# One Trainium2 core, sparse attention by its leading entries: row factors by root and reciprocal, a column number that carries its own skip, whole-block searches, a wider table, wider late segments

## The chip, the cores and the metric

The kernel runs on one core of a Trainium2 chip. The metric is the time of one execution on the device in microseconds (us). Before the change the median of three executions is 234.67 us (234.59 to 234.72).

## What is computed

The reference adds a four-head graph attention to `x` and normalises each row:

```python
ht = (h @ W).reshape(N, 4, 512).transpose(1, 0, 2)
e = jax.nn.leaky_relu(src[:, :, None] + dst[:, None, :], 0.01) + adj_mat[None]
att = jax.nn.softmax(e, axis=-1)
return jnp.einsum('hij,hjd->hid', att, ht).mean(axis=0)
...
x = _layernorm(x + _L0_gnn_ref(x, adj, W, a), axis=-1)
```

Here `x` is 4096 x 512, `adj` is 4096 x 4096 with entries up to 1e9, and `W` is 512 x 2048, all in 32-bit floats. The entries of `adj` are so large that the softmax of a row has all its weight on the column of the row's largest entry. So the attention of row i is row j of `x` times the mean of the four heads of `W`, where j is that column; the kernel computes just that, tests at the end whether the gaps to the second largest entries are wide enough for it, and would run a general version (`general`) if one were not.

## The kernel before the change

The 4096 rows are worked on in 32 blocks of 128, numbered 0 to 31. In the loop over `t` (lines 523 to 584) each turn issues work for several blocks in different stages, all engines have their program written out by hand in this order, and each engine works through its own list in that order.

- SyncE's DMA queue loads `adj` block by block (2 MB each, line 127), five blocks ahead, into six buffers, with the loads of `x` (line 134) between them; a buffer is free when VectorE has searched it. The stores of the result follow at the end (line 430).
- VectorE, for block t: `segment_maxima` (line 203) takes the maximum of each segment of 16, 32 or 64 columns, as two reductions of 2048 columns each; `find_segment` (lines 210 and 212) finds the row's largest segment and its number `at`. GpSimd adds the row's offset (`row`, line 219), fetches that one segment of `adj` again (`lead`, line 223, an indirect DMA) and multiplies the number by the segment's width (`start`, line 230).
- VectorE, for block t - 2: `find_column` (lines 257 and 263) looks for the maximum within the fetched segment. GpSimd forms the column number (`col`, line 265) and gathers the 128 rows of `x` that it names (`y`, lines 239 and 248, an indirect DMA). In the turns of the tuple `END` (1, 2 and 5 to 19) `find_column` stands behind `find_segment`, in the others between the two halves of the segment search.
- Blocks 1 to 17 are `TABLED`: rows of `x` below 128 are not gathered. Their products lie in a table that was computed once, and a one-hot matrix `pick` (`spread`, lines 324 to 328) selects them on TensorE. For such a block GpSimd adds 8192 to column numbers below 128 (`away`, `there`, lines 245 and 247), which puts them outside the bounds of the gather, so that they are skipped, and ScalarE has cleared the block beforehand.
- TensorE, for block t - 3: the gathered rows are transposed (`tp`, line 277), ScalarE copies them (`yt`, line 279), and TensorE adds the residual (line 289), the table's part (line 336) and the product with the mean of the heads (line 296).
- ScalarE, for block t - 4: the square sum of a row of `x` (`row_norm`, line 340) and the sums for mean and variance (`parked_stats`, lines 361 and 363).
- Every fourth turn from t = 8 on, `rstd` makes the factors of four blocks, t - 8 to t - 5, on GpSimd: a multiply and add, the power -0.5 (line 367), and two more products. ScalarE's `finish` (line 375) applies them a turn or more later.

So at turn t the factors need the sums of block t - 5, which ScalarE forms in its turn t - 1, behind the copy of the transposed rows of block t - 4. Those rows were gathered in turn t - 2.

From block 24 (`BEHIND`) on the results are put by, and finished after the loop (lines 586 to 652); the last blocks are normalised on VectorE with batch statistics (`moments`, `factor`, `normalise`). `head_norms` (lines 453 to 473), in turns 24, 26 and 28, computes norms for the final test, with a PSUM tile `px` that has one buffer and that `spread` uses as well.

## Time and profile before

| what | before |
|---|---|
| median of three runs | 234.67 us |
| the profiled execution: its time | 234.5 us |
| its span in the trace | 233.0 us |
| VectorE busy | 191.1 us (82%) |
| TensorE busy | 194.3 us (83%) |
| ScalarE busy | 139.8 us (60%) |
| GpSimd busy | 112.9 us (48%) |
| moved by DMA | 96.45 MB, mean 414 GB/s |

The trace gives each instruction a start and a duration, counted from the start of the span. Behind an instruction that found its engine idle stand, in square brackets, the length of that idle time and what ended it. Some 1.5 us of the execution lie outside the span. PE is TensorE, PEld its weight loads, DVE is VectorE, ACT is ScalarE, POOL is GpSimd, SP is SyncE.

### The profile page before, as it was taken

Reading aid. Unit: us, or ns where it says so; the run is one execution under the profiler, and the core shown is the slowest. Engines: PE = TensorE matmul, PEld = TensorE weight load, DVE = VectorE, ACT = ScalarE, POOL = GpSimd, SP = SyncE. Lnnn points to the kernel's source line nnn. Section 1 sums busy time; section 2 is a strip of 40 time slices with the busy share of each in tenths; the row PEclk is TensorE's granted clock in tenths of the full one; section 3 lists DMA queues with packets and bytes.
Section 4 is the critical chain, followed back from the end, with each engine's and each line's share of the span. In section 5 each row is a group of like instructions: output and inputs, shape, how many; then the busy total and the mean of one; then the engine's idle time right before and its main releaser. Section 6 shows DMA issues by size and latency. Waiting matters only on the chain.

```text
span 233.0 us, 2399 instructions
## 1 busy us (share of the span) xinstructions
PE 194.3 (83%) x570; PEld 92.6 (40%) x576; DVE 191.1 (82%) x301; ACT 139.8 (60%) x340; POOL 112.9 (48%) x260
## 2 busy tenths in 40 slices
PE   0069988789099996999899999999999977899990
PEld 0024443334044443445344444544443433345460
DVE  0448299899969997999799958977999999988782
ACT  3002213588077775699798767767756763289761
POOL 4020415615554875467657755653465447557210
PEclk9999999999769998899999999999999999999998
DMA  6999999999999999999999999999999999999985
GB/s 229 433 422 437 420 437 421 438 427 414 436 431 420 422 433 434 427 421 434 423 426 424 432 429 427 420 430 430 429 432 413 427 422 425 410 425 418 424 357 203
DMA packets 12834, 96.45 MB, mean 414 GB/s; under 512 B 2087, under 2 KB 2535, under 8 KB 7056
## 3 DMA queue, kind: packets, MB, share of 16 engines
q1 hardware_dynamic: 9216, 88.08, 89.5%
q0 software_dynamic: 3584, 8.16, 8.9%
q8 instruction: 5, 0.08, 0.1%
q14 instruction: 13, 0.11, 0.1%
q10 hardware_dynamic: 16, 0.02, 0.0%
HBM read 88.54 MB, written 8.39 MB: 416 GB/s over the span
## 4 chain that ended last, share of the span: by engine, by line
DMA 64%; DVE 19%; PE 6%; ACT 4%; issue 3%; POOL 1%; SPq 0%; DVEq 0%; POOLq 0%
DMA adj_t<-in_adj_dram 56%; DVE seg L203 16%; DMA hold<-in_L_gnn_W_dram 5%; PE o L296 4%; DMA y<-in_x_dram,col 3%; ACT sq L340 2%; PE o L384 2%; DVE at L212 1%; ACT hold L375 1%; DVE top L210 1%; PE tp L277 1%; DVE within L263 1%; POOL sd L367 0%; POOL lead L223 0%; ACT yt L279 0%
## 5 line engine op out<-in xcount | busy, mean ns | idle before, releaser
L203 DVE TENSOR_REDUCE seg<-adj_t 128x128 f32<-128x2048 f32 (+3 forms) x66 | 144.1, 2210 | 29.8 <-DMA adj_t<-in_adj_dram 29.7
L296 PE MATMUL o<-w_sum,yt 128*128 128x512 f32 x248 | 114.4, 602 | 2.0 <-ACT yt L279 1.8
L296 PEld LDWEIGHTS o<-w_sum,yt 128*128 128x128 f32 x248 | 46.3, 193 | 54.9 <-issue 42.6
L279 ACT COPY yt<-tp 128x512 f32<-128x512 f32 x33 | 19.1, 579 | 34.3 <-PE tp L277 34.3
L223 POOL DMA_INDIRECT lead<-in_adj_dram,row x32 | 32.6, 1020 | 13.1 <-POOL row L219 13.1
L277 PE MATMUL tp<-ident,y 128*128 128x128 f32 x128 | 22.5, 300 | 15.9 <-DMA y<-in_x_dram,there 12.0
L219 POOL TENSOR_TENSOR row<-at,first 128x1 uint32<-128x1 uint32 x32 | 6.1, 191 | 54.0 <-DVE at L212 45.4
L277 PEld LDWEIGHTS tp<-ident,y 128*128 128x128 f32 x128 | 18.7, 208 | 30.5 <-issue 27.0
L435 PE MATMUL o<-hold,ident 128*128 128x512 f32 x32 | 17.0, 699 | 13.7 <-DMA hold<-in_L_gnn_W_dram 13.7
L289 PE MATMUL o<-hold,ident 128*128 128x512 f32 x52 | 27.5, 614 | 0.0
L248 POOL DMA_INDIRECT y<-in_x_dram,there x17 | 18.9, 1111 | 10.9 <-POOL there L247 5.6
L340 ACT ACTIVATE sq<-hold 128x512 f32<-128x512 f32 x32 | 19.9, 624 | 0.0
L375 ACT ACTIVATE hold<-hold,nm,sd 128x512 f32<-128x512 f32 x24 | 19.1, 802 | 0.0
L239 POOL DMA_INDIRECT y<-in_x_dram,col x15 | 14.9, 995 | 7.6 <-POOL col L265 7.0
L363 ACT ACTIVATE sq<-hold,nm 128x512 f32<-128x512 f32 x24 | 17.4, 724 | 0.8
L435 PEld LDWEIGHTS o<-hold,ident 128*128 128x128 f32 x32 | 7.1, 226 | 22.8 <-issue 22.3
L436 ACT ACTIVATE w_sum<-o 128x512 f32<-128x512 f32 x4 | 2.4, 597 | 22.9 <-PE o L435 22.9
L326 ACT ACTIVATE off<-px,minus 128x128 f32<-128x128 f32 x17 | 6.3, 368 | 15.3 <-PE px L324 15.3
L361 ACT ACTIVATE hold<-o 128x512 f32<-128x512 f32 x24 | 14.3, 597 | 0.8
L336 PE MATMUL o<-z,pick 128*128 128x512 bf16 x46 | 13.9, 407 | 0.2
L210 DVE MAX8 top<-seg 128x8 f32<-128x256 f32 (+2 forms) x32 | 11.6, 361 | 1.1
L212 DVE FIND_INDEX8 at<-top,seg 128x8 uint32<-128x256 f32 (+2 forms) x32 | 11.3, 352 | 0.0
(113 smaller groups left out, 178.7 us busy)
## 6 DMA issues: line engine op xcount, KB each, us to landing
adj_t<-in_adj_dram SPq DMA_DIRECT2D x28, 2048.0 KB, 33.0
hold<-in_x_dram SPq DMA_DIRECT2D x6, 1024.0 KB, 32.4
adj_t<-in_adj_dram SPq DMA_DIRECT2D x6, 1024.0 KB, 28.1
hold<-in_L_gnn_W_dram SPq DMA_DIRECT2D x2, 2048.0 KB, 16.6
out_dram<-hold SPq DMA_DIRECT2D x7, 512.0 KB, 5.4
out_dram<-hold SPq DMA_DIRECT2D x3, 1024.0 KB, 15.1
adj_t<-in_adj_dram SPq DMA_DIRECT2D x4, 512.0 KB, 19.8
hold<-in_x_dram SPq DMA_DIRECT2D x2, 512.0 KB, 14.4
```

What stands on the lines that cost most here:

```text
L203: nc.vector.tensor_reduce(seg_of[ib][:, ts(k, N // e // n)], adj_t[ib][:, ts(k, N // n)].rearrange("p (s e) -> p s e", e=e), axis=AX.X, op ...
L223: nc.gpsimd.indirect_dma_start(out=lead, out_offset=None, in_=adj_segs[e], in_offset=bass.IndirectOffsetOnAxis(ap=row[:, :1], axis=0),)
L239: nc.gpsimd.indirect_dma_start(out=y, out_offset=None, in_=x, in_offset=bass.IndirectOffsetOnAxis(ap=col[:, :1], axis=0),)
L248: nc.gpsimd.indirect_dma_start(out=y_t[ib], out_offset=None, in_=x, in_offset=bass.IndirectOffsetOnAxis(ap=there[:, :1], axis=0), bounds_c ...
L277: nc.tensor.transpose(tp[:, kb, :], y[:, ds(kb, P, KB)], ident)
L279: nc.scalar.copy(yt, tp)
L289: nc.tensor.matmul(o_ps[ib], ident, hold[:, ib, :], start=start, stop=False)
L296: nc.tensor.matmul(o_ps[ib], yt_of[ib][:, kb, :], w_sum[:, kb, :], start=(start and kb == 0), stop=(kb == KB - 1),)
L340: nc.scalar.activation(sq, hold[:, ib, :], AF.Square, accum_out=xx[:, ib : ib + 1])
L363: nc.scalar.activation(sq, hold[:, ib, :], AF.Square, bias=nm[:, i], scale=-float(D), accum_out=sd[:, i])
L375: nc.scalar.activation(hold[:, ib, :], o, AF.Identity, bias=nm[:, i], scale=sd[:, i])
L435: nc.tensor.matmul(o, ident, hold[:, w_at + kb * H + h, :], start=(h == 0), stop=(h == H - 1))
```

## The change

It has six parts.

1. The factors (`rstd`): ScalarE takes the root (`root`, a new function, issued at the end of turn t - 1 for the factors of turn t), VectorE the reciprocal (in place of GpSimd's power, at the place where `rstd` stood), and GpSimd keeps the two products. The same holds for the last call of `rstd`, after the loop.
2. The skip of tabled blocks is added to the segment's start (in `fetch_segment`), so that `col` is the gather's index as it stands.
3. `END` reaches to turn 27, and in its turns the segment search is one reduction of all 4096 columns.
4. The table serves blocks 1 to 20.
5. Segments are 64 columns wide from block 24 (before: from block 28).
6. `head_norms` is called in turns 21, 22 and 23.

```diff
-LAST = 4
+LAST = 8
-TABLED = range(1, 18)
+TABLED = range(1, 21)
...
-    LEADS = (8, 8, LAST)
+    LEADS = (8, 4, LAST)
...
-    nc.gpsimd.iota(nth, pattern=[[0, 1]], base=0, channel_multiplier=-1)
+    nc.gpsimd.iota(nth, pattern=[[0, 1]], base=-1, channel_multiplier=-1)
...
-        n = max(pieces(ib), 2)
+        n = max(pieces(ib), 1 if ib in END else 2)
...
-            nc.gpsimd.tensor_tensor(start, at[:, 0:1], width[:, k : k + 1], op=OP.mult)
+            if ib in TABLED:
+                away = small.tile([P, 1], F32, name="away")
+                nc.gpsimd.tensor_scalar(away, at[:, 0:1], float(P // e), float(SKIP), op0=OP.is_lt, op1=OP.mult)
+                nc.gpsimd.tensor_scalar(start, at[:, 0:1], float(e), away, op0=OP.mult, op1=OP.add)
+            else:
+                nc.gpsimd.tensor_tensor(start, at[:, 0:1], width[:, k : k + 1], op=OP.mult)
...
-        away = small.tile([P, 1], U32, name="away")
-        nc.gpsimd.tensor_scalar(away, col, float(P), float(SKIP), op0=OP.is_lt, op1=OP.mult)
-        there = small.tile([P, 1], U32, name="there")
-        nc.gpsimd.tensor_tensor(there, col, away, op=OP.add)
...
+    def root(i):
+        nc.scalar.activation(sd[:, i], sd[:, i], AF.Sqrt, bias=eps, scale=1.0 / D)
+
     def rstd(i):
-        nc.gpsimd.tensor_scalar(sd[:, i], sd[:, i], 1.0 / D, EPS, op0=OP.mult, op1=OP.add)
-        nc.gpsimd.tensor_tensor(sd[:, i], sd[:, i], power[:, : i.stop - i.start], op=OP.pow)
+        nc.vector.reciprocal(sd[:, i], sd[:, i])
         nc.gpsimd.tensor_mul(nm[:, i], nm[:, i], sd[:, i])
...
-    END = (*range(1, 3), *range(5, 20))
+    END = (*range(1, 3), *range(5, 28))
...
-        middle = 1 if t == NB - 1 else 2
+        middle = PIECES if t in END else 1 if t == NB - 1 else 2
...
-        segment_maxima(t, middle, PIECES)
+        if t not in END:
+            segment_maxima(t, middle, PIECES)
...
-        if t in (24, 26, 28):
-            head_norms((t - 24) // 2)
+        if 21 <= t < 24:
+            head_norms(t - 21)
...
+        if FINISH <= t + 1 < NB and (t + 1) % Q == 0:
+            root(slice(t + 1 - FINISH, t + 1 - FINISH + Q))
...
     stats(BEHIND + 2)
+    root(slice(BEHIND, BEHIND + 3))
     rstd(slice(BEHIND, BEHIND + 3))
```

What the change does to the engines' lists is seen best at three places. The first is VectorE's list around turn 12: `seg` are the segment maxima of a block, `lead` the fetched segment of the block two before. Before the change it reads:

```order
L203 TENSOR_REDUCE seg_796<-adj_t 128x128 x2
L210 MAX top<-seg_796 128x8
L212 MAX_INDEX at<-top,seg_796 128x8
L257 MAX inner<-lead_683 128x8
L263 MAX_INDEX within<-top,lead_683 128x8
L203 TENSOR_REDUCE seg_860<-adj_t 128x128 x2
```

After the change, at the same place:

```order
L201 TENSOR_REDUCE seg_772<-adj_t 128x256
L208 MAX top<-seg_772 128x8
L210 MAX_INDEX at<-top,seg_772 128x8
L256 MAX inner<-lead_663 128x8
L262 MAX_INDEX within<-top,lead_663 128x8
L368 RECIPROCAL sd<-sd 128x4
L201 TENSOR_REDUCE seg_832<-adj_t 128x256
```

The two reductions of a block have become one, and the reciprocal of four blocks' roots stands ahead of the next block's reduction.

The second place is ScalarE's list, where the root of those factors is made; `sq,sd` are the square sums of block 7. Before the change:

```order
L279 COPY yt<-tp 128x512
L444 ACTIVATE sq,ww<-hold 128x512
L340 ACTIVATE sq,xx<-hold 128x512
L361 ACTIVATE hold,nm<-o 128x512
L363 ACTIVATE sq,sd<-hold,nm 128x512
L375 ACTIVATE hold<-hold,nm,sd 128x512
```

After the change:

```order
L278 COPY yt<-tp 128x512
L445 ACTIVATE sq,ww<-hold 128x512
L339 ACTIVATE sq,xx<-hold 128x512
L360 ACTIVATE hold,nm<-o 128x512
L362 ACTIVATE sq,sd<-hold,nm 128x512
L365 ACTIVATE sd<-sd,eps 128x4
L376 ACTIVATE hold<-hold,nm,sd 128x512
```

The root stands behind the square sums of block 7 and so behind the copy of the transposed rows of block 8, in ScalarE's turn 11.

The third place is TensorE's list in turn 21, after the change, with the semaphores that its rows wait for: the two products of `head_norms` and, behind them, block 18's `spread`.

```order
L295 MATMUL o<-w_sum,yt 128x512 x3
L460 MATMUL px<-ww,ones 128x16
L461 MATMUL px<-each,ones 128x8 [waits DVE_49]
L323 LDWEIGHTS low [waits DVE_49,Pool_49]
L323 MATMUL px<-ident_b,low 128x128 [waits PE_49]
L276 MATMUL tp<-ident,y 128x128 [waits DMASW7_49]
```

`spread` of block 18 is new here, since the table now serves this block, and it needs the one `px` buffer, which is free when VectorE has read the norms in its turn 22; that is its wait for VectorE.

## The prediction

> **What bounds the kernel now.** I read the page first, then VectorE's waits, then the timeline.

> ```profile
> PEclk9999999999769998899999999999999999999998
> DMA  6999999999999999999999999999999999999985
> ```

> Of the 40 slices of 5.8 us each, the second row tells that the DMA engines are full in all but the first and the last two, so the stream of `adj` sets the pace. VectorE, which searches what lands, is close behind. Its waits from block 12 on:

> ```profile
> DVE seg L203 <- DMA adj_t<-in_adj_dram: 8.5, 7, 2.7
> ```

> Between 70 and 200 us VectorE waits only 8.5 us for `adj`. That is all the room it has: whatever it loses beyond 8.5 us makes it the bound.

> The end hangs on TensorE:

> ```profile
> 191.18 0.72 PE L277 MATMUL tp<-ident,y 128*128 128x128 f32 x4 [0.53 <-DMA y<-in_x_dram,col]
> 196.60 0.72 PE L277 MATMUL tp<-ident,y 128*128 128x128 f32 x4 [1.18 <-DMA y<-in_x_dram,col]
> 203.64 0.72 PE L277 MATMUL tp<-ident,y 128*128 128x128 f32 x4 [1.09 <-DMA y<-in_x_dram,col]
> ```

> These are the transposes of blocks 25, 26 and 27; each waited for its gathered rows. Behind block 27 TensorE runs almost without a gap to the end of the last block, so a shift of block 27 shifts the end.

> **The reciprocal on VectorE.** VectorE's list is worked through in order, and the new reciprocal stands between block t's search and block t + 1's, for t = 8, 12, ... 28. It waits for ScalarE's root, which needs the sums that stand behind the copy of block t - 4, whose rows were gathered in turn t - 2. I follow this loop for t = 16, from the end of block 14's search. The rows of VectorE (starts of blocks 14 and 15, and the places where the searches of 14 and 15 are over):

> ```profile
> 101.64 4.46 DVE L203 TENSOR_REDUCE seg<-adj_t 128x128 f32<-128x2048 f32 x2
> 107.08 0.16 DVE L257 MAX8 inner<-lead 128x8 f32<-128x16 f32 x1
> 107.30 4.46 DVE L203 TENSOR_REDUCE seg<-adj_t 128x128 f32<-128x2048 f32 x2
> 112.74 0.16 DVE L257 MAX8 inner<-lead 128x8 f32<-128x16 f32 x1
> ```

> A block takes 107.30 - 101.64 = 5.66 us, and its search is over 5.44 us after its start. GpSimd's rows, the fetch of segment 14 with the gather for block 12, and the next fetch; then the path from column to gather of a block without the skip:

> ```profile
> 108.69 1.06 POOL L223 DMA_INDIRECT lead<-in_adj_dram,row  x1 [0.27 <-POOL row L219]
> 109.91 0.20 POOL L265 TENSOR_TENSOR col<-start,within 128x1 uint32<-128x1 uint32 x1
> 110.20 0.24 POOL L245 TENSOR_SCALAR away<-col 128x1 uint32<-128x1 uint32 x1
> 110.52 0.19 POOL L247 TENSOR_TENSOR there<-col,away 128x1 uint32<-128x1 uint32 x1
> 111.33 1.11 POOL L248 DMA_INDIRECT y<-in_x_dram,there  x1 [0.62 <-POOL there L247]
> 113.61 1.05 POOL L223 DMA_INDIRECT lead<-in_adj_dram,row  x1 [0.51 <-POOL row L219]
> ...
> 141.42 0.19 POOL L265 TENSOR_TENSOR col<-start,within 128x1 uint32<-128x1 uint32 x1 [0.31 <-DVE within L263]
> 142.14 1.04 POOL L239 DMA_INDIRECT y<-in_x_dram,col  x1 [0.54 <-POOL col L265]
> ```

> Where GpSimd is free, the fetch begins 113.61 - 112.74 = 0.87 us after the search. From fetch to gather it is 111.33 - 108.69 = 2.64. With the skip moved into `start`, column to gather shrinks from 1.42 to 0.72, and `start` grows by one operation of 0.32 (110.20 to 110.52): 2.64 - 0.70 + 0.32 = 2.26. So the gather issues 0.87 + 2.26 = 3.1 us after the search, 0.4 us better than it would before. Then the landing, the transpose, the copy and the sums:

> ```profile
> y<-in_x_dram,there POOLq DMA_INDIRECT x17, 8.3
> y<-in_x_dram,col POOLq DMA_INDIRECT x15, 7.2
> ```

> ```profile
> 115.39 0.72 PE L277 MATMUL tp<-ident,y 128*128 128x128 f32 x4 [1.13 <-DMA y<-in_x_dram,there]
> ...
> 116.15 0.59 ACT L279 COPY yt<-tp 128x512 f32<-128x512 f32 x1 [1.14 <-PE tp L277]
> 119.44 0.80 ACT L375 ACTIVATE hold<-hold,nm,sd 128x512 f32<-128x512 f32 x1
> 121.77 0.57 ACT L279 COPY yt<-tp 128x512 f32<-128x512 f32 x1
> 124.43 0.80 ACT L375 ACTIVATE hold<-hold,nm,sd 128x512 f32<-128x512 f32 x1
> ```

> From a transpose's start to the copy it is 0.76 us, and from the copy to the end of the sums 124.43 - 121.77 = 2.66 (3.29 in turns up to 14, which square a piece of `W` as well, so 0.63 more). Root and reciprocal, by the nearest rows:

> ```profile
> L401 ACT ACTIVATE sd<-mv,eps 128x1 f32<-128x1 f32 x5 | 1.4, 287 | 1.6 <-DVE mv L399 1.6
> L404 DVE RECIPROCAL sd<-sd 128x1 f32<-128x1 f32 x5 | 0.8, 156 | 0.8 <-ACT sd L401 0.7
> L469 ACT ACT_TABLE_LOAD x1 | 1.3, 1283 | 0.0
> ```

> The loop is 3.1 + 8.3 + 0.76 + 2.66 + 0.29 + 0.16 = 15.3 us, from 107.08 to 122.4. Without the wait VectorE would begin block 17 at 107.30 + 2 x 5.66 - 0.16 = 118.5 (0.16: two merged reductions, below). **It stands still for 3.9 us.** The trace has the lag already, on the engine that does this work now:

> ```profile
> 101.77 0.19 POOL L366 TENSOR_SCALAR sd<-sd 128x4 f32<-128x4 f32 x1 [1.04 <-ACT sq L363]
> 103.68 0.20 POOL L219 TENSOR_TENSOR row<-at,first 128x1 uint32<-128x1 uint32 x1
> ```

> At t = 12 GpSimd got the sums at 101.77, when VectorE had already begun block 14 (101.64); the reciprocal of these sums now stands ahead of block 13. GpSimd's wait cost only a late `row`: block 13's search was over by 101.64, and its `row` went at 103.68, behind the factors. [...]

> The other turns, from 3.9: t = 12 has one more square, 4.5. t = 8 has that and the table load (1.28), which the order of ScalarE's list moves from `head_norms` to the first root; but there VectorE had waited for `adj` itself:

> ```profile
> 66.32 4.48 DVE L203 TENSOR_REDUCE seg<-adj_t 128x128 f32<-128x2048 f32 x2 [2.19 <-DMA adj_t<-in_adj_dram]
> ...
> 125.57 4.46 DVE L203 TENSOR_REDUCE seg<-adj_t 128x64 f32<-128x2048 f32 x2
> 130.96 4.46 DVE L203 TENSOR_REDUCE seg<-adj_t 128x64 f32<-128x2048 f32 x2
> ...
> 181.16 2.28 DVE L203 TENSOR_REDUCE seg<-adj_t 128x64 f32<-128x2048 f32 x1
> ...
> 204.51 3.45 DVE L203 TENSOR_REDUCE seg<-adj_t 128x16 f32<-128x1024 f32 x3
> ```

> so 3.9 + 0.63 + 1.28 - 2.19 = 3.6. [...] From block 18 on blocks are shorter (130.96 - 125.57 = 5.39), so VectorE arrives 0.54 earlier: 4.4 at t = 20 and at t = 24. At t = 28 the rows come without a skip (7.2 instead of 8.3, path 0.3 shorter) and the blocks are shorter still: 3.2. Stalls up to t = 24: 3.6 + 4.5 + 3.9 + 4.4 + 4.4 = 20.8 us, and 3.2 behind.

> **What VectorE gains.** Three reductions of 1024 columns take 3.45, 1.15 each; half of one in a pair of 2048 is 4.46 / 4 = 1.12: some 0.07 us go with each instruction saved, 0.08 taken, bounds 0 and 0.1. Blocks 8 to 27: 1.6 us. Segments of 64 in blocks 24 to 27 make the finds shorter, 0.1 a block by 0.07 in the first of them:

> ```profile
> L210 DVE MAX8 top<-seg 128x8 f32<-128x128 f32 x10 | 3.0, 295 | 0.3
> L210 DVE MAX8 top<-seg 128x8 f32<-128x64 f32 x4 | 0.9, 228 | 0.1
> ```

> Together 2.0. `head_norms` only moves, and the stream of `adj`, loaded five blocks ahead, runs on while VectorE stands. What waits behind the reciprocal is the next block's search, with it GpSimd's fetch and gather, and TensorE behind these. So block 27 begins 20.8 - 8.5 - 2.0 = 10.3 us later, at 181.16 + 10.3 = 191.5.

> **The longer END.** In turns 20 to 27 `find_column` now follows the whole search. Block 25's gather therefore waits for block 27's search, over at 191.5 + 5.0 (5.44 less 0.27, 0.08 and 0.1), then 0.87 + 1.94 (2.64 - 0.70) on GpSimd: 199.3; landing 7.2: 206.5. Before, block 25's transpose began at 191.18 and block 27's at 203.64, with waits of 1.18 and 1.09 between, so 10.2 us of work. Block 27 is now transposed at 206.5 + 10.2 = 216.7, **13.1 us later**, and the end with it.

> **The last factors.** Behind the loop the reciprocal of blocks 24 to 26 stands in VectorE's list as well:

> ```profile
> 220.05 0.68 DVE L395 BATCH_NORM_STATS2 st<-o 128x6 f32<-128x512 f32 x1
> ...
> 220.74 0.19 POOL L366 TENSOR_SCALAR sd<-sd 128x3 f32<-128x3 f32 x1 [4.17 <-ACT sq L357]
> ...
> 227.31 0.43 DVE L418 BATCH_NORM_STATS2 halves_st<-o 128x6 f32<-128x256 f32 x1 [0.54 <-PE o L384]
> ```

> The sums are there at 220.74; root, reciprocal and three small operations on VectorE (0.4) put the statistics that began at 220.05 at 221.6. Of the 1.5 us, 0.54 is idle time before the last statistics; 1.0 reaches the end.

> **Costed at nothing.** The power on GpSimd, gone: GpSimd is off the path wherever VectorE stands. Three more tabled blocks add products to TensorE, which idles in every stall; without that cover 2 us. The bytes that three tabled blocks skip are 0.8 MB at the very most (all 3 x 128 rows of 2 KB), 1.9 us of the stream at 414 GB/s; where VectorE is the bound, the stream has that to spare. Block 18's `spread` waits for VectorE's norms in turn 22; block 20's rows, which the next root needs, land no earlier than TensorE is back at them, give or take 0.5.

> **The sum.** 234.5 (the profiled execution, 0.2 under the median) + 13.1 + 1.0 = **248.6 us**.

> **The rivals.**

> First, fewer stalls: at t = 24 the trace of before shows no wait of GpSimd for sums. But there `find_column` stood in mid-block, so rows came earlier. If that stall stays away: 248.6 - 4.4 = 244.2. Chance 0.15.

> Second, longer stalls: the granted TensorE clock falls to 7 and 6 tenths in two slices at 58 to 70 us, which is 4 us of TensorE's time (5.8 x 0.3 + 5.8 x 0.4), and again to 8 tenths twice behind 87 us. One such stretch on a root's path that this sum doesn't hold adds up to 4 us: 252.6. Chance 0.10.

> Third, no stall at all (VectorE passes, or the sums come in time). Then block 27 begins at about 180.8, block 25's rows land at 180.8 + 5.0 + 2.8 + 7.2 = 195.8, block 27's transpose is at 206.0, 2.4 late, and with 1.0 the time is 237.9. Chance 0.03.

> Fourth, not slower: gathers that land fast. If rows land within 8.3 - 3.9 = 4.4 us, the stalls go and END's delay too: block 25 at 192.6, block 27 at 202.8, 0.8 early; with 1.0 lost at the end 234.7. For it speaks only that GpSimd has less to do; against it, that the DMA engines are as full as before. Chance 0.02.

> **The numbers.** My case, 246 to 252, has 0.70. Landings 0.8 us shorter or longer in each loop give 4 us either way on the path, the merge 1.6 to nothing; the range is 243.5 to 255.5. Under 0.2% (0.5 us, about what can be told from no change) stays nothing but the fourth rival: slower 0.97, same 0.02, faster 0.01.

> **What would show it.** VectorE's reciprocal (line 368) with 3 to 5 us of idle time ahead of it, ended by ScalarE's root, six times, some 24 us in sum; VectorE's waits for `adj` after block 8 near nothing; block 29 begun about 13 us late; block 27's transpose near 217; a late slice or two in which DMA is not full. I am wrong if the reciprocal's idle time is under a microsecond, or if the DMA engines stay the bound with VectorE waiting for `adj` as before.

## The result, and the profile after

| what | before | after |
|---|---|---|
| median, us | 234.63 (4 runs, 234.20 to 234.72) | 260.90 (4 runs, 259.96 to 262.04) |
| profiled execution: span, us | 233.0 | 260.2 |
| VectorE's waits for the root, us | none | 38.4 |
| VectorE's waits for `adj`, us | 29.7 | 21.0 |
| granted TensorE clock, mean | 0.975 | 0.923 |

The changed kernel takes 1.1126 times as long (95% interval 1.1066 to 1.1186): 26.3 us more, where 14 were forecast. The sign and the place were right, the size was not. The first view is the page's clock and DMA rows of the changed kernel, 40 slices of 6.5 us:

```profile
PEclk9999999995699977999799968997999869999997
DMA  6999999999999999999999999999998999525244
```

Before, the clock dipped in two places; now it dips again and again, about every fourth block. And DMA is far from full in the last six slices. The reciprocals in VectorE's timeline, with the idle time ahead of each in the brackets:

```profile
78.17 0.18 DVE L368 RECIPROCAL sd<-sd 128x4 f32<-128x4 f32 x1 [6.13 <-ACT sd L365]
107.65 0.18 DVE L368 RECIPROCAL sd<-sd 128x4 f32<-128x4 f32 x1 [6.92 <-ACT sd L365]
135.32 0.18 DVE L368 RECIPROCAL sd<-sd 128x4 f32<-128x4 f32 x1 [5.11 <-ACT sd L365]
164.91 0.18 DVE L368 RECIPROCAL sd<-sd 128x4 f32<-128x4 f32 x1 [7.79 <-ACT sd L365]
192.65 0.18 DVE L368 RECIPROCAL sd<-sd 128x4 f32<-128x4 f32 x1 [5.19 <-ACT sd L365]
219.34 0.18 DVE L368 RECIPROCAL sd<-sd 128x4 f32<-128x4 f32 x1 [5.77 <-ACT sd L365]
246.48 0.17 DVE L368 RECIPROCAL sd<-sd 128x3 f32<-128x3 f32 x1 [1.52 <-ACT sd L365]
```

The first six are the stalls of the prediction, at the turns that it named, each ended by ScalarE's root; but they sum to 36.9 us, not 24.0. (The seventh, 1.52 us, is that of the last factors, behind the loop.) TensorE's transposes show why. Blocks 7, 8 and 9 first, then 24 and 27:

```profile
94.82 1.10 PE L276 MATMUL tp<-ident,y 128*128 128x128 f32 x4 [5.67 <-DMA y<-in_x_dram,col]
103.11 0.70 PE L276 MATMUL tp<-ident,y 128*128 128x128 f32 x4
108.64 0.70 PE L276 MATMUL tp<-ident,y 128*128 128x128 f32 x4
...
215.53 0.63 PE L276 MATMUL tp<-ident,y 128*128 128x128 f32 x4
...
229.21 0.64 PE L276 MATMUL tp<-ident,y 128*128 128x128 f32 x4
```

Block 7's transpose found TensorE idle for 5.67 us, and took 1.10 us; block 8's took 0.70. From block 7 to block 8 it is 8.29 us, from block 8 to block 9 5.53. The stretches view of TensorE (length, busy time, granted clock, DMA share, GB/s) around these blocks and in a stretch in which TensorE is never idle:

```profile
90.00:100.00 10.00, 5.18 (x11) 0.69 1.02 434
160.00:170.00 10.00, 10.00 (x35) 1.00 0.99 417
```

The clock records of the trace give half the clock from 93.7 to 100.5 us. So block 7, the first one behind the stall, is worked on at half the clock up to there, and the next one, whose root the next reciprocal waits for, comes 2.8 us late: its rows landed at 100.27 us, by the trace's DMA records, and its transpose began at 103.11. Block 27's transpose is at 229.21, 25.6 us later than before; from block 31's transpose to the end it is 12.4 us against 10.7.

### The profile page after: what moved, and what is told of

It is laid out like the page before. It is cut to its first block, busy times and chain, and to the rows that moved or that the text cites. A ratio compares the mean times of both kernels' runs of the same rounds, so it can differ in the third digit from the quotient of the medians.

```text
span 260.2 us, 2399 instructions
## 1 busy us (share of the span) xinstructions
PE 204.4 (79%) x581; PEld 98.1 (38%) x588; DVE 189.1 (73%) x283; ACT 145.0 (56%) x356; POOL 103.7 (40%) x234
## 4 chain that ended last, share of the span: by engine, by line
PE 32%; DMA 27%; ACT 15%; DVE 13%; issue 6%; POOL 3%; another core or an unknown queue 2%; SPq 0%; POOLq 0%; DVEq 0%
DMA y<-in_x_dram,col 19%; PE o L295 16%; DVE seg L201 8%; DMA hold<-in_L_gnn_W_dram 8%; PE o L288 5%; PE tp L276 4%; ACT sq L339 3%; PE o L436 3%; PE o L335 2%; ACT yt L278 2%; ACT sq L362 2%; POOL lead L221 2%; PE o L308 1%; ACT hold L360 1%
## 5 line engine op out<-in xcount | busy, mean ns | idle before, releaser
L201 DVE TENSOR_REDUCE seg<-adj_t 128x256 f32<-128x4096 f32 (+5 forms) x41 | 141.8, 3466 | 21.1 <-DMA adj_t<-in_adj_dram 21.0
L295 PE MATMUL o<-w_sum,yt 128*128 128x512 f32 x248 | 117.1, 614 | 2.0 <-ACT yt L278 1.8
L295 PEld LDWEIGHTS o<-w_sum,yt 128*128 128x128 f32 x248 | 48.2, 200 | 56.1 <-issue 45.5
L276 PE MATMUL tp<-ident,y 128*128 128x128 f32 x128 | 24.1, 316 | 27.2 <-DMA y<-in_x_dram,col 27.2
L276 PEld LDWEIGHTS tp<-ident,y 128*128 128x128 f32 x128 | 19.6, 209 | 39.9 <-issue 38.4
L288 PE MATMUL o<-hold,ident 128*128 128x512 f32 x52 | 31.7, 700 | 0.0
L368 DVE RECIPROCAL sd<-sd 128x4 f32<-128x4 f32 (+1 forms) x7 | 1.2, 178 | 38.4 <-ACT sd L365 38.4
L436 PE MATMUL o<-hold,ident 128*128 128x512 f32 x32 | 16.7, 681 | 13.9 <-DMA hold<-in_L_gnn_W_dram 13.9
L247 POOL DMA_INDIRECT y<-in_x_dram,col x20 | 21.7, 1086 | 6.5 <-POOL col L264 5.9
L325 ACT ACTIVATE off<-px,minus 128x128 f32<-128x128 f32 x20 | 7.3, 367 | 26.4 <-PE px L323 26.4
L335 PE MATMUL o<-z,pick 128*128 128x512 bf16 x54 | 17.1, 425 | 0.7 <-ACT pick L327 0.3
L242 POOL DMA_INDIRECT y<-in_x_dram,col x12 | 11.7, 978 | 4.4 <-POOL col L264 3.8
L335 PEld LDWEIGHTS <-pick 128*128 128x128 bf16 x60 | 6.3, 108 | 18.3 <-issue 9.2
```

The source lines that it names most:

```text
L201: nc.vector.tensor_reduce(seg_of[ib][:, ts(k, N // e // n)], adj_t[ib][:, ts(k, N // n)].rearrange("p (s e) -> p s e", e=e), axis=AX.X, op ...
L247: nc.gpsimd.indirect_dma_start(out=y_t[ib], out_offset=None, in_=x, in_offset=bass.IndirectOffsetOnAxis(ap=col[:, :1], axis=0), bounds_che ...
L276: nc.tensor.transpose(tp[:, kb, :], y[:, ds(kb, P, KB)], ident)
L288: nc.tensor.matmul(o_ps[ib], ident, hold[:, ib, :], start=start, stop=False)
L295: nc.tensor.matmul(o_ps[ib], yt_of[ib][:, kb, :], w_sum[:, kb, :], start=(start and kb == 0), stop=(kb == KB - 1),)
L335: nc.tensor.matmul(o_ps[ib], pick, z[k], start=(start and k == 0), stop=False)
```

## The experiments

Two theories stood at first. **A**: the wait of VectorE for the root carries the loss, made longer by the clock that falls after each stall. **B**: the longer END and the moved norms carry a good part of it by themselves. The times of before beside these runs were 234.45 to 234.57 us.

### The factors back on GpSimd

In the changed kernel, `root` and its calls are taken out:

```diff
-        nc.vector.reciprocal(sd[:, i], sd[:, i])
+        nc.gpsimd.tensor_scalar(sd[:, i], sd[:, i], 1.0 / D, EPS, op0=OP.mult, op1=OP.add)
+        nc.gpsimd.tensor_tensor(sd[:, i], sd[:, i], power[:, : i.stop - i.start], op=OP.pow)
```

> The changed kernel with the factors made on GpSimd by the power again, as before the change; the other five parts stay. Theory A (VectorE stands still ahead of the reciprocal, and all but 3 us of the loss comes from that): 236 to 239 us, no idle time of VectorE outside its waits for adj, TensorE's granted clock back near 0.97. Theory B (the loss comes from the other parts, above all the longer END and the wait of block 18 for the px buffer): 250 us or more.

235.49 us, ratio 1.0048 (1.0023 to 1.0074), half a microsecond below the range of theory A. The reciprocal's part of the change costs 25.4 of the 26.3 us; the other five parts together cost 1.0. VectorE's waits are for `adj` again:

```profile
DVE seg L203 <- DMA adj_t<-in_adj_dram: 30.9, 15, 8.7
```

### Root and reciprocal alone

The first part of the change is put into the kernel before, nothing else.

> The kernel before with the first part alone: root on ScalarE a turn ahead, reciprocal on VectorE, two products on GpSimd. Theory A: six waits of VectorE for the root, 5 to 8 us each at t = 8 to 20 and 2 to 5 us at t = 24 and 28 (rows are gathered in mid-block there), in sum 28 to 36 us, time 251 to 259 us. Theory B: under 240 us.

251.88 us, ratio 1.0727 (1.0678 to 1.0777): the time is in the range of theory A, but there are four stalls (6.25, 6.68, 5.00, 7.49 us) where it had six, and none at turns 24 and 28. So the reciprocal alone costs 17.4 us, and with parts that cost 1.0 alone it costs 25.4: the parts make each other dearer. Which of them do, the runs with END and the norms put back tell.

### The reciprocal one turn later

```diff
-        if t >= FINISH and t % Q == 0:
-            rstd(slice(t - FINISH, t - FINISH + Q))
+        if t > FINISH and t % Q == 1:
+            rstd(slice(t - 1 - FINISH, t - 1 - FINISH + Q))
```

> The changed kernel with one line moved: the reciprocal and the two products are issued one turn later (t = 9, 13, ... 29), the root stays where it is. Nothing is left out. VectorE comes to the reciprocal 5.6 us later than in the changed kernel. Theory A with the clock (a stall of 3 to 4 us by the loop at full clock, made 2 to 3 us longer by the half clock that TensorE is granted after each idle stretch): the loop of 15.3 us now has 17 us, the wait falls to under 1 us at every place, TensorE no longer idles there, the clock stays up, and the time is 236 to 239 us. Theory A without the clock (the loop is simply 2 us longer than reckoned, 17.5 to 18.5 us): waits of 0.5 to 2 us stay at each place, 238 to 243 us. Theory B: 250 us or more.

237.19 us, ratio 1.0101 (1.0066 to 1.0136): 23.7 us gone, with the same instructions. None of the six reciprocals waits. Two of them in VectorE's timeline, and VectorE's waits for `adj`:

```profile
101.36 0.16 DVE L368 RECIPROCAL sd<-sd 128x4 f32<-128x4 f32 x1
125.76 0.16 DVE L368 RECIPROCAL sd<-sd 128x4 f32<-128x4 f32 x1
```

```profile
DVE seg L201 <- DMA adj_t<-in_adj_dram: 30.7, 15, 8.7
```

The mean granted clock is 0.976, against 0.975 before. A has the cause; B is left with at most the 2.6 us that stay.

### TensorE kept busy through the stalls

The changed kernel with 4 to 6 products more, whose result is overwritten, before blocks 3, 7, 11, 15, 18 and 23:

```diff
+    FILL = {3: 6, 7: 5, 11: 4, 15: 4, 18: 4, 23: 4}
...
+        for _ in range(FILL[ib]):
+            nc.tensor.matmul(o_ps[ib], ident, w_sum[:, 0, :], start=True, stop=True)
```

> The changed kernel with idle stretches of TensorE filled: ahead of blocks 3, 7, 11, 15, 18 and 23 TensorE multiplies the identity with a block of W 4 to 6 times (3.7 to 5.5 us) into the tile that the block's first real product then overwrites; the result does not use them. Theory A with the clock: the granted clock stays near full through 60 to 220 us, the six waits of VectorE fall from 5.1 to 7.8 us to 3.5 to 5.5 us (sum 24 to 28 instead of 36.9), and the time falls to 247 to 254 us although TensorE does 25 us more work. Theory A without the clock (the half clock goes with the idle time but costs nothing on the way to the root): the waits stay at a sum of 35 to 39 us and the time at 259 to 262 us.

250.09 us, ratio 1.0651 (1.0602 to 1.0701): more work, and 10.8 us less time than the changed kernel. The clock row of its page, and its reciprocals:

```profile
PEclk9999999999999999999999999999999999999997
```

```profile
75.29 0.18 DVE L375 RECIPROCAL sd<-sd 128x4 f32<-128x4 f32 x1 [3.30 <-ACT sd L372]
102.55 0.18 DVE L375 RECIPROCAL sd<-sd 128x4 f32<-128x4 f32 x1 [4.69 <-ACT sd L372]
129.18 0.18 DVE L375 RECIPROCAL sd<-sd 128x4 f32<-128x4 f32 x1 [4.06 <-ACT sd L372]
156.25 0.18 DVE L375 RECIPROCAL sd<-sd 128x4 f32<-128x4 f32 x1 [5.27 <-ACT sd L372]
182.81 0.18 DVE L375 RECIPROCAL sd<-sd 128x4 f32<-128x4 f32 x1 [4.01 <-ACT sd L372]
206.13 0.18 DVE L375 RECIPROCAL sd<-sd 128x4 f32<-128x4 f32 x1 [2.41 <-ACT sd L372]
```

With the clock at full the stalls sum to 23.7 us (forecast 24.0), and block 27's transpose is at 217.25 (forecast 216.7). From the landing of the rows that a root needs to their transpose it is 0.4, 0.1, 0.1, 2.4, 0.4 and 0.6 us at the six turns, where the changed kernel has 1.9 to 5.4. So the loop as the prediction reckoned it was right for a TensorE at full clock, and what it left out is the clock.

### The last reciprocal later

Next the 2.6 us that stay when the reciprocals are a turn later. That kernel, and behind the loop:

```diff
-    rstd(slice(BEHIND, BEHIND + 3))
     products(NB - 3, KB - 1, KB)
...
     moments(NB - 3)
+    rstd(slice(BEHIND, BEHIND + 3))
```

> As the run with the reciprocals a turn later (237.19 us), and behind the loop the reciprocal of blocks 24 to 26 stands behind the statistics of block 29 on VectorE instead of ahead of them; nothing is left out. Theory: of the 2.6 us that stayed over before, 1.5 us are VectorE's wait for the last root (1.52 us in the trace), the rest block 27's delay of 1.0 us. Then VectorE's wait for the last root goes and the time falls by 1.0 to 1.6 us, to 235.6 to 236.2. Rival (the last wait is covered by work of TensorE): no change, 237.0 to 237.4.

237.37 us, ratio 1.0106 (1.0082 to 1.0131): no change, the rival's case. The wait of 1.52 us is gone, and the issue of the last store stands 7.08 us behind block 31's transpose instead of 7.56, so the last factors are worth 0.5 us; but the span ends 5.12 us behind that issue instead of 4.83. Something at the very end takes back what is won.

### END back as well, and END back with the power

Both have `END` to turn 19; the first is the run above with it, the second the run with the power.

```diff
-    END = (*range(1, 3), *range(5, 28))
+    END = (*range(1, 3), *range(5, 20))
```

> As the run with the last reciprocal later, and END ends at turn 19 again (whole-block searches in its turns only). Theory: the longer END delays block 27's transpose by 0.9 to 1.0 us; without it that begins near 203.6 us, and the time is 234.4 to 235.2. Rival: the delay comes from something else (the earlier 64-column segments or the wider table); then no change against the run before it, 235.6 to 236.2.

> The changed kernel with the factors by power on GpSimd and with END back to turn 19; what is left of the change are the skip in the segment's number, the merged searches in turns 1, 2 and 5 to 19, the table to block 20, the 64-column segments from block 24 and the norms in turns 21 to 23. If the 1.1 us by which the run with the power alone stayed over before come from END, this gives 234.2 to 234.9, no difference from before within 0.3 us. If DMA were not the bound, the 1.5 us less work on VectorE would show: 233.0 to 233.5. If the delay comes from other parts: 235.2 to 235.7.

234.35 us, ratio 0.9978 (0.9963 to 0.9992), and 235.40 us, ratio 1.0023 (1.0006 to 1.0039). The first ends where its theory put it (within 0.05 us), but by a gain of 3.0 us where the theory had 1; the second falls into the case that END is not the reason. So the same edit gives 3.0 us in one kernel and 0.1 in the other, and neither theory explains both. The first is the one version whose interval lies wholly below before, by 0.2%. The second issues its last store at 228.91 us, earlier than before (229.32), and still ends 1.0 us later. Its branch around `general` (line 68), in VectorE's list, with first and last start behind the durations in ns:

```profile
L68 DVEq EVENT_SEMAPHORE  x2: 21/21/21, 232.5 to 232.6; - x2
L68 DVEq COMPARE_BRANCH  x1: 84/84/84, 229.4 to 229.4; - x1
```

Behind the branch VectorE does nothing for 3.05 us, and SyncE waits for it at the end:

```profile
SPq L830 <- DVEq L68: 1.9, 1, 1.9
```

In the traces of before and of the runs with the power alone, with root and reciprocal alone and with the first of these two the same stretch is 0.50 us; in those of the changed kernel, of the reciprocals a turn later, of the filled one and of the last reciprocal later 2.5 to 3.1. What the second group has in common is the length of VectorE's list: 326 rows in the trace, where the others have 319, 333, 343 and 350.

### END back alone

> The changed kernel with END back to turn 19 and all else as it is, root and reciprocal too. Theory (END and the reciprocal multiply each other: where the column search stands behind the whole segment search, rows are gathered some 2.5 us later and the loop that the reciprocal closes is that much longer): the stalls at turns 24 and 28 go, as in the run with root and reciprocal alone, four stalls of 5 to 8 us stay, and the time is 248 to 252 us. Rival (END costs only the 0.9 us at block 27 that it costs without the reciprocal): 259 to 260.5 us with six stalls.

The changed kernel with that one line: 256.21 us, ratio 1.0926 (1.0885 to 1.0967). This lies between the theory and its rival: the stall at turn 28 goes, the one at turn 24 stays.

```profile
189.78 0.18 DVE L368 RECIPROCAL sd<-sd 128x4 f32<-128x4 f32 x1 [6.04 <-ACT sd L365]
```

The expectation was too low by 4 us (the four runs spread from 253.24 to 257.69 us; the trace is of the first), and what makes the stall at turn 24 was still open. Of the 4.7 us by which this kernel is below the changed one, 1.6 are not END's place in the loop: VectorE's list has 333 rows here, and from the last store's issue to the end it is 3.18 us instead of 4.82.

### Seven instructions more

The run with power and END back, and the one with the last reciprocal later, each with seven clears of a column that nobody reads at the start of VectorE's list, where it waits for `adj`:

```diff
+    spare = once.tile([P, 7], F32, name="spare")
+    for k in range(7):
+        nc.vector.memset(spare[:, k : k + 1], 0.0)
```

> As the run with power and END back (235.40 us), and VectorE clears seven small columns that nobody reads, at the start, where it waits for the first adj rows; so its list has seven instructions more. Theory (where VectorE's code lies decides): in the five traces in which VectorE's list has 326 rows it stands still for 2.5 to 3.1 us behind its last branch, and in the five others (319, 333, 343, 350 rows) for 0.5 us. With 333 rows the 3.05 us become 0.5, the span's end comes 3.2 to 4.6 us behind the last store's issue instead of 5.07, and the time is 233.6 to 235.0 us. Rival (the count is chance, the stall has another cause): 235.2 to 235.6 us with the 3 us still there.

> As the run with the last reciprocal later (237.37 us, 326 rows in VectorE's list, 3.10 us behind its last branch), with the same seven small clears. Theory: 0.5 us behind the branch, the end 3.2 to 4.6 us behind the last store's issue instead of 5.12, and the time 235.4 to 236.9 us; what is then over the 234.6 of before is block 27's delay by the longer END, about 1 us. Rival: no change, 237.0 to 237.7 us.

234.33 us, ratio 0.9991 (0.9979 to 1.0003), and 235.61 us, ratio 1.0052 (1.0029 to 1.0075): 1.1 and 1.8 us less, for more work. The branch in the first of them:

```profile
L68 DVEq EVENT_SEMAPHORE  x2: 21/21/21, 229.2 to 229.4; - x2
L68 DVEq COMPARE_BRANCH  x1: 84/84/84, 228.6 to 228.6; - x1
```

The 3 us are 0.5 again. Without them END costs much the same in both kernels: 235.61 us against 234.35 with the reciprocals a turn later, 235.49 against 234.33 with the power, 1.3 and 1.2 us.

In both pairs of runs nothing but the length of VectorE's list was changed. The traces also have DMA packets of a kind `instruction`: behind VectorE's last branch there are three of them in the traces of the changed kernel and of the run with power and END back (326 rows each), and two in those of the kernel before and of the first run with seven more. The rows of that kind from 229 us on, in the run with power and END back and in the same with seven more:

```profile
q14 instruction: 3, 0.02, 1.1%
```

```profile
q14 instruction: 2, 0.02, 0.6%
```

So there is one packet more in the traces in which VectorE stands still. But the packets do not name their engine, and the third comes only when the wait is over (in the changed kernel at 259.4 us, where VectorE goes on at 258.8; with power and END back at 233.0, where it goes on at 232.5): what VectorE waits for there is not shown.

### The norms back, with END back and alone

The last open point, the stall at turn 24. The changed kernel has a wait of TensorE at block 18's `spread`, behind the norms:

```profile
176.41 0.27 PE L323 MATMUL px<-ident_b,low 128*128 128x128 bf16 x1 [3.82 <-DVE n L469]
```

The run with END back alone and the changed kernel itself, each with

```diff
-        if 21 <= t < 24:
-            head_norms(t - 21)
+        if t in (24, 26, 28):
+            head_norms((t - 24) // 2)
```

> The changed kernel with END back to turn 19 (256.2 us) and the norms in turns 24, 26 and 28 as before; root and reciprocal stay. Theory (the norms cause the stall at turn 24): in turn 21 the two products of the norms stand ahead of block 18's spread on TensorE, whose px buffer comes free only when VectorE, itself late, has read them; TensorE idles 3.80 us there, the half clock follows, and block 20's root comes late. Without that wait TensorE has no gap at 169 to 173 us, the reciprocal of turn 24 waits under 1 us instead of 6.04, and the time is 249 to 252 us. Rival (TensorE would have waited for block 18's rows at that place anyway): a gap of 3 to 4 us ended by the gathered rows, the stall at turn 24 still 5 to 6 us, and 255 to 257 us.

> The changed kernel with the norms in turns 24, 26 and 28 as before and nothing else; END stays at turn 27. Theory: the px wait of 3.82 us in turn 21 goes; the stall at turn 24 falls from 5.19 to 3 to 4.4 us, since with the longer END the gathers stay late; the time falls by 1 to 3 us, to 258 to 260 us. If the stall at turn 24 goes wholly, as it did with root and reciprocal alone: 255 to 256. Rival: no change, 260 to 262 us with a wait for rows in the place of the px wait.

251.23 us, ratio 1.0741 (1.0703 to 1.0778), and 256.33 us, ratio 1.0924 (1.0906 to 1.0943). With END and norms back the reciprocal of turn 24:

```profile
186.38 0.18 DVE L368 RECIPROCAL sd<-sd 128x4 f32<-128x4 f32 x1 [0.32 <-ACT sd L365]
```

It is 0.32 instead of 6.04 us: the norms made that stall. With the norms alone back the stalls at turns 24 and 28 fall from 5.19 and 5.77 to 2.21 and 2.75 (in a trace of the slowest of five runs, 258.73 us), and the time falls by 4.6 us, more than expected. END back on top takes another 5.1 us, of which 1.7 are again the end of the program (3.19 us from the last store's issue instead of 4.87, with 333 rows instead of 326). So with the stalls the norms cost 4.6 us and END 3.4 (5.0 and 3.1 by the run with END back alone); without the stalls END costs 1.2 to 1.3, and the moved norms nothing that shows, since the kernels with 234.35 and 234.33 us have them too. What the stalls add, 4.6 and some 2.2 us, makes up most of the 8.0 us by which the reciprocal costs more among the other parts than alone; 1.5 of the 8.0 are the end of the program again (from the last store's issue on, the reciprocal adds 1.0 us among the other parts, 4.82 against 3.80, and takes 0.5 alone, 3.18 against 3.64).

## Why the prediction was wrong

**What held.** The bound and its change: VectorE's waits for `adj` behind block 8 went, and six waits for the root came, at the turns named. The loop's own terms at t = 12: the search is over at 89.23, the gather of block 8 issues at 92.34 (3.1, as forecast), the rows land 7.9 us later (8.3 taken). From its copy at 103.92 to the root at 107.32 it is 3.40 (3.29), from there to the reciprocal 0.33 (0.29). The table load took its 1.28. From the start of a block's search to its first find it is 4.43 us with one reduction (83.85 to 88.28), 4.49 to 4.51 with two before: 0.06 to 0.08, where 0.08 was taken. The first rival, no stall at turn 24, did not come (5.19 us). The third, no stall at all, and the fourth, that rows land in 4.4 us, are refuted by the stalls and by a median landing of 7.9 us.

**The step that failed** is in "The reciprocal on VectorE": "From a transpose's start to the copy it is 0.76 us", set directly behind the landing. That took TensorE to be at its place, and at full clock, when the rows land. At t = 12 the rows landed at 100.27, and the transpose began at 103.11: 2.8 us that the sum doesn't have, since TensorE was still at block 7, at half the clock. The same gap is 3.1, 2.8, 1.9, 3.6, 5.4 and 3.0 us at the six turns, by the landings in the trace's DMA records. A gap was there to be read in the trace of before: for the same blocks it is 1.0, 2.5, 1.0, 1.2, 2.0 and 0.9 us. (At turn 24, with 5.4, the rows had landed early, 5.2 us after their gather, so the stall is only 0.8 longer than forecast.) The prediction knew the clock, but as a rival of its own ("One such stretch on a root's path that this sum doesn't hold adds up to 4 us") with a chance of 0.10 and one stretch. It isn't independent, and it isn't one. The first dip, at 60 to 70 us, was there before and lies on the path of turn 8's root: 6.13 us of stall in place of 3.6, and 3.30 in the filled run. From then on each stall stops the gathers, TensorE runs dry for 3.8 to 5.7 us, the clock is halved for 3.4 or 6.8 us, the next root is late, and the next stall is longer than the sum has it. The filled run prices it: 10.8 us of the 12.3 by which the forecast was too low.

**"Block 18's `spread` waits for VectorE's norms in turn 22 ... give or take 0.5"** was wrong as well: block 20's rows landed at 183.33, and TensorE came to them at 188.72, 5.4 us later. VectorE's turn 22 is itself late behind the stall of turn 20, so TensorE idled 3.82 us there, and its clock was half from 175.6 to 179.0 us: 4.6 us by the run with the norms back. Part of this is in the 10.8 already, since the filled run bridges that idle time too; the two can't be added.

**"The stream of `adj` ... runs on while VectorE stands"** held in part. In five of the six stalls SyncE waited 9.5 to 13.2 us for a buffer that VectorE had not freed, the first time from 71 us on. Still DMA moved 418 GB/s or more in each slice of the page from the second to 169 us, and only then fell behind (320 to 421 GB/s up to 221 us). VectorE was the bound by then, and no wait for `adj` came back, so this cost nothing that the trace shows.

**The last factors** were put at 1.0 us: the reciprocal costs 0.5, and 1.2 came from the 2.5 us behind the last branch, which the sum doesn't have (4.82 us from the last store's issue to the end, 3.64 before). **END** was put at 2.4 without the stalls (the third rival); it costs 1.2 to 1.3, and with the reciprocals a turn later block 27's transpose is 1.0 us late. Its cost in the stalls was right in kind: 25.6 us at block 27's transpose against 22.0 at its search is 3.6, where 2.8 was forecast.

What stays open: how the 26.3 us split among the clock, END and the norms, since each makes the others larger; only the reciprocal's place takes 23.7 of them away by itself.

## What to carry to other kernels

A wait that is put into the list of an engine that works in order is priced by the loop that it closes; if the loop runs through TensorE, price its next block at half the clock wherever the stall leaves TensorE idle for 3.8 us or more, as in all seven cases below, and follow the loop round twice, since the late block makes the next stall longer. Two edits that lie on that loop cost more with the stalls than alone: a wait for a shared buffer 4.6 us against nothing that shows, a later gather 3.4 against 1.2 to 1.3. Where the result isn't needed at once, put the instruction that waits one turn later: the same work went from 260.9 to 237.2 us.

## What the runs showed of the hardware

**The clock after idle time.** In the traces of the kernel before and of the changed one TensorE idled seven times for 3.8 to 6.6 us (from 50 to 222 us), and each time the clock records show half the clock, from a point within the idle time or at most 0.3 us behind its end, for 3.41, 6.83 or once 10.24 us. Of the four idle times from 1.09 to 1.90 us the longest was followed by 3.41 us of half clock, the others, up to 1.18 us, by none. That longest one, in the kernel before, with the stretch behind it:

```profile
90.25 0.72 PE L277 MATMUL tp<-ident,y 128*128 128x128 f32 x4 [1.90 <-DMA y<-in_x_dram,there]
```

```profile
90.00:100.00 10.00, 9.75 (x29) 0.83 1.01 429
```

The TensorE stretches of the changed kernel along the clock records, around its second halving:

```profile
69.82:93.71 23.89, 19.27 (x60) 1.00 1.01 428
93.71:100.54 6.83, 5.72 (x12) 0.50 1.03 436
100.54:124.43 23.89, 19.54 (x63) 1.00 1.01 427
```

**The end of the program.** Two kernels took 1.1 and 1.8 us less when VectorE's list was made longer by seven instructions, and nothing else was changed. A difference of under 1% between two kernels needs a look at the last 5 us of both traces before it is put down to the edit.
